# Selective scan: two of sixteen states take their product with B from GpSimd instead of VectorE

## The chip, the core and the metric

The kernel runs on one core of a Trainium2 chip. The metric is the device time of one execution in microseconds (us); less is better.

## The reference

Four layers, each a mixer and a feed-forward part with residuals, on four images of 64 x 64 positions and 96 channels. Layer 0 has a gated recurrence of its own. Layers 1 to 3 share a selective scan over four orders of the positions (row by row, column by column, and both backwards), 192 inner channels and 16 states per channel. Cut to what the change touches:

```python
# per layer 1..3; xs: [image, 4 orders, 192 channels, 4096 positions]
dts, B, C = split(x_proj(xs))            # B, C: 16 rows for each order, the same for all channels
delta = softplus(dt_proj(dts) + bias)
for t in range(4096):                    # for every image, order, channel and state n
    h[n] = exp(delta[t] * A[n]) * h[n] + (delta[t] * u[t]) * B[n, t]
    y[t] = sum_n(h[n] * C[n, t])
y = y + D * u
```

Afterwards the four orders are added, normalised, gated with silu(z) and projected out; the feed-forward part works in an 8-bit float format.

## The kernel before

**Stages.** Layer 0 runs first (function `gated`, to about 1800 us). Then `scans` works through 12 stages (4 images x 3 layers), and at the end the last image's output part runs alone. The work between two scans of an image (projections, convolution, norms, feed-forward) is cut into small steps by generators (`between`, `Job`, `Chain`), which the scan loop pumps beside its own work.

**Tiles of the scan.** A stage has two directions, four segments of T = 1024 positions each, and three chunks; a chunk fills 128 partitions with 64 channels of one order and 64 channels of another. So there are 12 x 2 x 4 x 3 = 288 chunks (`Item`), each with 16 states: 4608 state tiles of 128 x 1024 in float32. The list `tiles` holds them in order, and the loop over k takes one state a step.

**One state on the engines.**
- ScalarE: `decays` writes `da = exp(delta * A[n])` to SBUF (three buffers), two states ahead.
- TensorE: `b_rows` spreads B's row n over the partitions, two matmuls of a selection matrix `sel` with `bs` (B in three bfloat16 parts), into the PSUM tile `bc` from `wide()` (two buffers), one state ahead.
- VectorE, in `scan`: a product `bc = du * bc` in place (`du = delta * u`), then `beside()`, which pumps the other work, then the scan instruction `h <- da, carry, bc`.
- SyncE: `c_rows` starts two transfers that spread C's row out of the DRAM tile `cs` over 64 partitions each, two states ahead, into one of six buffers `c`.
- ScalarE: `carry` saves the last column of h. GpSimd: `times_c` makes `c = h * c`, one state behind.
- TensorE: `accumulate`, three states behind, adds h * C into the PSUM tile `acc`, which sums the 16 states of a chunk; `keep_busy` fills TensorE with idle matmuls (`nothing`) up to 1536 columns a step. `take` copies a full `acc` out on ScalarE four states behind the last state, that is in the step of state 3 of the next chunk, ahead of that step's other ScalarE work.

**Order.** Every engine is wrapped in `InOrder`: its instructions run in the order in which the program issues them. Within a step the order is `take`, `carry`, `c_rows`, `decays`, `logarithms` (at state 11), `b_rows`, `times_c`, `scan` with `beside`, `store`, `accumulate`. `logarithms` takes the logarithm of all variances that wait in `pending`; with the exponentials around it that costs ScalarE a table load before and one after. `prepare_chunk` makes delta (softplus, at state 4) and du (on GpSimd) of the next chunk; `prepare_segment` makes the rows of B and C, every third chunk, and stores C's rows to `cs`.

**Buffers.** PSUM holds two `bc` tiles of two banks, two banks for the other work and `acc` with two. The SBUF tile `e` is used in layer 0 alone.

All instructions carry the line of the wrapper `InOrder.call` in the profile (L91), so groups are told apart by their tiles.

Of the kernel before, what the change touches and what calls it, by code (L numbers as in the profile page):

```python
# [10 lines left out]
F32 = mybir.dt.float32  # L11
# [4 lines left out]
ALU = mybir.AluOpType  # L16
# [5 lines left out]
NS = 16  # L22
# [3 lines left out]
T = 1024  # L26
MM = 512
# [11 lines left out]
NC2 = 2 * NS  # L39
# [26 lines left out]


FILL = 1536


def columns(lhs, rhs, place):
# [45 lines left out]
def metaformer(ctx: ExitStack, tc: tile.TileContext, x, l0_ab, l0_rest, ssm, ffn, out):  # L117
    nc = tc.nc
    pe, act, dve, pool, sp = (
        InOrder(tc, e) for e in (nc.tensor, nc.scalar, nc.vector, nc.gpsimd, nc.sync)  # L120
    )
# [3 lines left out]
    dram = ctx.enter_context(tc.tile_pool(name="dram", bufs=6, space=bass.MemoryType.DRAM))  # L125
    pbc = ctx.enter_context(tc.tile_pool(name="pbc", bufs=2, space=bass.MemoryType.PSUM))

    def sb(bufs, tag, shape, dtype=F32):
        return pools[bufs].tile(shape, dtype, tag=tag, name=tag)

    def const(name, shape, dtype=F32):
        return pools[1].tile(shape, dtype, name=name)
# [3 lines left out]
    def wide():  # L136
        return wides[0].tile([128, T], F32, tag="bc", name="bc")
# [4 lines left out]
    def bank(name):  # L142
        banks["free"] -= 1
        return banks["pool"].tile([128, MM], F32, tag="ps", name=name)

    def release():
        banks["back"] += 1

    def settle():
        banks["free"] += banks["back"]  # L150
        banks["back"] = 0
# [16 lines left out]
    def drain(chain, others=lambda: None, until=lambda: False):  # L168

        while chain is not None and not chain.done and not until():  # L170
            if not pump(chain):
                others()
            settle()
# [41 lines left out]
    for layer in range(4):  # L215
# [8 lines left out]
        b = const(f"b_{layer}", [128, 3 + C])  # L224
# [558 lines left out]
    def load_segment(item):  # L783
        sg = Segment()
        t = slice(item.seg * T, (item.seg + 1) * T)
        sg.steps = False
        sg.us = [sb(4, "u", [128, T]) for _ in range(3)]
        for c in range(3):
            sp.dma_start(out=sg.us[c], in_=item.im.u[c, :, t])
        weights[item.layer].load_xp()  # L790
        sg.bs = sb(2, "bs", [NB3, T], BF16)
        sg.cs = dram.tile([NC2, T], F32, tag="cs", name="cs")
        return sg

    def prepare_segment(item, sg):

        xp = weights[item.layer].xp
        rows = sg.rows = sb(1, "rows", [128, T])
        for k in range(2):
            cols = slice(k * MM, (k + 1) * MM)  # L800
            ps = bank("x_proj")
            for c in range(3):
                o = (3 * item.d + c) * XPW
                pe.matmul(
                    ps[0:XPW], xp[:, o : o + XPW], sg.us[c][:, cols], start=c == 0, stop=c == 2
                )
                if c:
                    yield

            bs = sg.bs[:, cols]  # L810
            act.copy(rows[0:XPW, cols], ps[0:XPW])
            sg.steps = k == 1
            act.copy(bs[0:32], ps[0:32])
            yield
            rem = rows[64:96, cols]
            dve.tensor_tensor(rem, ps[0:32], bs[0:32], ALU.subtract)
            release()
            yield
            for p in (32, 64):
                act.copy(bs[p : p + 32], rem)  # L820
            yield k == 0
        sp.dma_start(out=sg.cs, in_=rows[NC2 : 2 * NC2])
        pool.tensor_tensor(sg.bs[64:96], rows[64:96], sg.bs[64:96], ALU.subtract)

    def prepare_chunk(item):
# [33 lines left out]
    def scans(stages, jobs, pac):  # L859
# [10 lines left out]
        sg = load_segment(items[0])  # L870
# [4 lines left out]
        tiles = [(i, n) for i in items for n in range(NS)]  # L875
        last = len(tiles) - 1
        live = {}
# [3 lines left out]
        def start(i):  # L881
# [2 lines left out]
                pool.memset(carries[i.chunk], 0.0)  # L884
            i.carry = carries[i.chunk]

        def c_rows(k):
            i, n = tiles[k]
            c = live[k, "c"] = sb(6, "c", [128, T])
            for half in range(2):  # L890
                row = NS * half + n
                sp.dma_start(
                    out=c[64 * half : 64 * half + 64],
                    in_=i.sg.cs[row : row + 1, :].to_broadcast([64, T]),
                )

        def decays(k):
            i, n = tiles[k]
            da = live[k, "da"] = sb(3, "da", [128, T])
            at = (3 * i.d + i.chunk) * NS + n  # L900
            act.activation(da, i.delta, AF.Exp, scale=weights[i.layer].decay[:, at : at + 1])

        def b_rows(k):
            i, n = tiles[k]
            b = live[k, "b"] = wide()
            for half in range(2):
                cols = slice(half * MM, (half + 1) * MM)
                pe.matmul(
                    b[:, cols], sel[:, n, :], i.sg.bs[:, cols], start=True, stop=True
                )  # L910

        def scan(k, beside):
            i, n = tiles[k]
            da, b = live.pop((k, "da")), live.pop((k, "b"))
            dve.tensor_tensor(b, i.du, b, ALU.mult)
            beside()
            h = live[k, "h"] = sb(3, "h", [128, T])
            step = slice(None, None, -1 if i.d else 1)
            dve.tensor_tensor_scan(
                h[:, step],  # L920
                da[:, step],
                b[:, step],
                initial=i.carry[:, n : n + 1],
                op0=ALU.mult,
                op1=ALU.add,
            )
# [49 lines left out]
        def take(i):  # L976
            i.y = sb(2, "y", [128, T])
            act.copy(i.y, i.acc)
# [15 lines left out]
        decays(0)  # L994
        decays(1)
        b_rows(0)
        working = []

        def work():

            while working and working[0].done:
                working.pop(0)
            if working:
                working[0].step()

        for k in range(last + 5):
            q, n = divmod(k, NS)
            if k <= last:
                item = items[q]
                nxt = at(q + 1)  # L1010
                if n == 0:
                    if q % per == 0:
                        item.im.y = dram.tile([3, 128, L], F32, tag="y", name="y")
                        working += jobs[q // per]
                    if item.chunk == 2:
                        drain(segment, work, lambda: nxt.sg.steps)
                    chain = Chain(prepare_chunk(nxt), True) if nxt is not None else None
                if item.chunk == 1 and n == 4 and at(q + 2) is not None:
                    if q % per == per - 2:
                        for job in jobs[q // per][:1]:  # L1020
                            while not job.done:
                                work()
                                settle()
                    segment = Chain(next_segment(items[q + 2 : q + 5]))
                if n == 8 and nxt is not None:
                    start(nxt)
                if n == 8 and nxt is not None and nxt.d == 1:
                    nxt.yf = sb(2, "y", [128, T])
                    sp.dma_start(out=nxt.yf, in_=nxt.im.y[nxt.chunk, :, nxt.seg * T : (nxt.seg + 1) * T])
            def beside():  # L1030
                pump(chain)
                pump(segment)
                if n == 13:
                    drain(chain, work)
                    if item.chunk == 2:
                        drain(segment, work)
                work()

            full = items[(k - 4) // NS] if k >= 4 and (k - 4) % NS == NS - 1 else None
            if full is not None:  # L1040
                take(full)
            if 0 <= k - 1 <= last:
                carry(k - 1)
            if k + 2 <= last:
                c_rows(k + 2)
                decays(k + 2)
            if n == 11:
                logarithms()
            if k + 1 <= last:
                b_rows(k + 1)  # L1050
            if 0 <= k - 1 <= last:
                times_c(k - 1)
            before = pe.columns
            if k <= last:
                scan(k, beside)
            if full is not None:
                store(full)
            if 0 <= k - 3 <= last:
                fill = max(0, FILL - int(pe.columns - before)) // MM
                if tiles[k - 3][1] == NS - 1:  # L1060
                    keep_busy(tiles[k - 3][0], fill)
                accumulate(k - 3)
                if tiles[k - 3][1] < NS - 1:
                    keep_busy(tiles[k - 3][0], fill)
            settle()
# [380 lines left out]
```

## Time and profile before

| | |
|---|---|
| median of three runs | 19232.42 us (19219.73 to 19237.42) |
| the profiled execution | 19237.79 us, its span 19236.0 us |
| VectorE busy | 17678.3 us, 92% |
| TensorE matmuls busy | 15881.9 us, 83% |
| GpSimd busy | 13540.9 us, 70% |
| ScalarE busy | 11070.3 us, 58% |
| DMA | 3192.77 MB, mean 166 GB/s |
| mean granted TensorE clock | 0.906 |

A group of the profile reads: engine, operation, written tile <- read tiles, partitions x elements, count | busy time in us, mean duration of one in ns | idle time of the engine just ahead of them, and what ended it. PE is TensorE, PEld its weight loads, DVE VectorE, ACT ScalarE, POOL GpSimd, SP SyncE. The table by stretches gives for each engine busy us and number of instructions, then the granted clock of TensorE, the busy share of the DMA engines and GB/s. In the timeline a row has start and duration in us; what is in brackets is the idle time before it and who ended it.

### The profile page before, as it was taken

What the parts mean: (1) busy time and instruction counts of PE and PEld (TensorE: products, weight loads), DVE (VectorE), ACT (ScalarE), POOL (GpSimd) and SP (SyncE); (2) the same over time, 40 slices, a digit from 0 to 9 for tenths busy, and PEclk for the clock granted to TensorE, in tenths of its full rate; (3) what the DMA queues carried; (4) which work ended last, traced back from release to release, by engine and by line L of the source; (5) the groups of instructions that cost most, each with busy time, mean ns of one, the idle gap of its engine ahead of it and who ended that gap; (6) DMA issues with size and microseconds to landing.
All of it is one profiled execution on the core that took longest, in us unless ns stands there. A gap on an engine that the chain in (4) does not pass through costs nothing.

```text
span 19236.0 us, 231374 instructions
## 1 busy us (share of the span) xinstructions
PE 15881.9 (83%) x75043; PEld 4903.2 (25%) x75043; DVE 17678.3 (92%) x13768; ACT 11070.3 (58%) x17831; POOL 13540.9 (70%) x9223
## 2 busy tenths in 40 slices
PE   8998787787787888888887888887887888788887
PEld 3332121121122222222222222222222222223333
DVE  6757999999999999999999999999999999999995
ACT  3544564564555665665665665665665665666664
POOL 3434777777777777777777777777777777777775
PEclk9999999998999899898899898899898898898887
DMA  1213676676676667666667677667666676676674
GB/s 50 54 45 86 165 190 174 169 190 170 170 189 178 172 186 185 173 186 184 172 186 183 171 190 184 170 188 187 170 192 181 169 194 179 170 196 176 171 182 114
DMA packets 1269891, 3192.77 MB, mean 166 GB/s; under 512 B 440336, under 2 KB 440560, under 8 KB 1262544
## 3 DMA queue, kind: packets, MB, share of 16 engines
q1 hardware_dynamic: 1268688, 3177.97, 62.4%
q8 instruction: 604, 9.90, 0.2%
q14 instruction: 599, 4.91, 0.1%
HBM read 2818.51 MB, written 308.28 MB: 163 GB/s over the span
## 4 chain that ended last, share of the span: by engine, by line
DVE 62%; PE 17%; ACT 10%; issue 4%; POOL 3%; DMA 2%; SPq 1%; DVEq 1%; POOLq 0%; ACTq 0%
DVE h L91 43%; DVE bc L91 17%; ACT da L91 5%; PE acc L91 5%; PE bc L91 4%; ACT L91 2%; PE conv L91 1%; POOL c L91 1%; PE dt_proj L91 1%; DMA c<-cs 1%; PE c L91 1%; DVE st L91 1%; PE y_t L91 1%; POOL du L91 1%; SPq L91 1%
## 5 line engine op out<-in xcount | busy, mean ns | idle before, releaser
L91 POOL TENSOR_TENSOR c<-h,c 128x1024 f32<-128x1024 f32 (+1 forms) x4992 | 11344.4, 2275 | 5043.9 <-DVE h L91 3032.8
L91 DVE TENSOR_TENSOR_SCAN h<-da,carry,bc 128x1024 f32<-128x1024 f32 x4608 | 10796.2, 2343 | 543.1 <-POOL c L91 38.1
L91 ACT ACTIVATE da<-delta,decay 128x1024 f32<-128x1024 f32 x4608 | 5286.8, 1148 | 1696.4 <-DVE h L91 1689.8
L91 DVE TENSOR_TENSOR bc<-du,bc 128x1024 f32<-128x1024 f32 x4608 | 5563.1, 1207 | 187.9 <-PE bc L91 177.2
L91 PE MATMUL acc<-c,twice 64*64 64x512 f32 x36864 | 5586.9, 679 | 27.0 <-POOL c L91 27.0
L91 PE MATMUL bc<-bs,sel 96*128 96x512 bf16 x9216 | 3042.3, 415 | 2801.7 <-DVE h L91 2729.7
L91 ACT COPY carry<-h 128x1 f32<-128x1 f32 x3456 | 653.2, 189 | 3983.4 <-DVE h L91 3980.3
L91 PEld LDWEIGHTS <-sel 96*128 96x128 bf16 x9216 | 593.7, 100 | 6162.0 <-DVE h L91 5068.6
L91 PE MATMUL acc<-sel,nothing 96*128 96x512 bf16 x5795 | 1728.8, 404 | 0.0
L91 PEld LDWEIGHTS acc<-c,twice 64*64 64x64 f32 x36864 | 1060.0, 142 | 2460.7 <-issue 1897.0
L91 ACT ACT_TABLE_LOAD x1287 | 1651.2, 1283 | 37.9 <-DVE mv L91 20.0
L91 PEld LDWEIGHTS <-nothing 96*128 96x128 bf16 x5795 | 417.7, 100 | 2143.5 <-issue 1957.9
L91 PE MATMUL conv<-pad,tap_lo 128*128 128x512 f32 x1728 | 880.8, 615 | 0.0
L91 PE MATMUL dt_proj<-rows,w 12*128 12x512 f32 x1152 | 747.5, 732 | 6.8 <-ACT delta L91 4.3
L91 ACT COPY y<-acc 128x1024 f32<-128x1024 f32 x288 | 291.6, 1013 | 762.3 <-PE acc L91 750.7
L91 POOL TENSOR_TENSOR du<-delta,u 128x1024 f32<-128x1024 f32 x288 | 679.3, 2359 | 1.5 <-issue 1.5
L91 ACT ACTIVATE c<-c,l_bias 128x512 f32<-128x512 f32 x384 | 263.6, 686 | 673.4 <-PE c L91 670.7
L91 PE MATMUL x_proj<-u,xp 128*108 128x512 f32 x1152 | 587.1, 619 | 19.0 <-DMA xp<-in_ssm 9.3
L91 PE MATMUL conv<-pad,tap_hi 128*128 128x512 f32 (+1 forms) x1152 | 602.6, 626 | 0.0
L91 DVE TENSOR_TENSOR_SCAN h<-da,l_carry,bc 128x512 f32<-128x512 f32 x384 | 491.3, 1280 | 41.9 <-DVE bc L91 1.4
L91 PE MATMUL bc<-rows,u 96*128 96x512 f32 x768 | 399.1, 645 | 42.5 <-DVE h L91 42.5
L91 PE MATMUL bc<-xp,u 96*128 96x512 f32 x768 | 395.5, 640 | 25.9 <-DVE h L91 25.9
(146 smaller groups left out, 12895.3 us busy)
## 6 DMA issues: line engine op xcount, KB each, us to landing
c<-cs SPq DMA_DIRECT2D x9216, 256.0 KB, 4.2
u<-u SPq DMA_DIRECT2D x288, 512.0 KB, 6.8
y<-y SPq DMA_DIRECT2D x1152, 128.0 KB, 3.5
y<-y SPq DMA_DIRECT2D x144, 512.0 KB, 6.1
xr<-x SPq DMA_DIRECT2D x224, 192.0 KB, 5.0
u<-u SPq DMA_DIRECT2D x288, 128.0 KB, 3.8
pad<-y SPq DMA_DIRECT2D x288, 128.0 KB, 4.7
z<-zl SPq DMA_DIRECT2D x96, 256.0 KB, 4.6
```

The lines of the kernel that those rows point to most:

```text
L91: ins = f(*a, **k).ins
```

## The change

States 4 and 12 of every chunk (`ON_POOL`) go another way. B's rows are stored to `cs` too, which is twice as large. For these states SyncE spreads B's row out of DRAM into the SBUF tile `e` (one buffer), five states ahead (`b_from_dram`); GpSimd multiplies it with du in place (`times_b_on_pool`), two states ahead and behind the product with C of that step; ScalarE writes the decay to a PSUM tile from `wide()`, in the place that `bc` had, one state ahead and behind the next state's decay (and at state 11 behind the logarithms); the broadcast matmuls and VectorE's product are gone. The scan reads its decay from PSUM and its product from SBUF. In the step before such a state the columns that `keep_busy` fills up to are 1024 fewer.

```diff
--- before.py
+++ after.py
@@ -66,6 +66,7 @@
 
 
 FILL = 1536
+ON_POOL = (4, 12)
 
 
 def columns(lhs, rhs, place):
@@ -789,7 +790,7 @@
             sp.dma_start(out=sg.us[c], in_=item.im.u[c, :, t])
         weights[item.layer].load_xp()
         sg.bs = sb(2, "bs", [NB3, T], BF16)
-        sg.cs = dram.tile([NC2, T], F32, tag="cs", name="cs")
+        sg.cs = dram.tile([2 * NC2, T], F32, tag="cs", name="cs")
         return sg
 
     def prepare_segment(item, sg):
@@ -819,7 +820,7 @@
             for p in (32, 64):
                 act.copy(bs[p : p + 32], rem)
             yield k == 0
-        sp.dma_start(out=sg.cs, in_=rows[NC2 : 2 * NC2])
+        sp.dma_start(out=sg.cs, in_=rows[0 : 2 * NC2])
         pool.tensor_tensor(sg.bs[64:96], rows[64:96], sg.bs[64:96], ALU.subtract)
 
     def prepare_chunk(item):
@@ -884,19 +885,35 @@
                 pool.memset(carries[i.chunk], 0.0)
             i.carry = carries[i.chunk]
 
+        def on_pool(k):
+            return 0 <= k <= last and tiles[k][1] in ON_POOL
+
+        def rows_of(i, first, dst):
+            for half in range(2):
+                row = first + NS * half
+                sp.dma_start(
+                    out=dst[64 * half : 64 * half + 64],
+                    in_=i.sg.cs[row : row + 1, :].to_broadcast([64, T]),
+                )
+
         def c_rows(k):
             i, n = tiles[k]
             c = live[k, "c"] = sb(6, "c", [128, T])
-            for half in range(2):
-                row = NS * half + n
-                sp.dma_start(
-                    out=c[64 * half : 64 * half + 64],
-                    in_=i.sg.cs[row : row + 1, :].to_broadcast([64, T]),
-                )
+            rows_of(i, NC2 + n, c)
+
+        def b_from_dram(k):
+            i, n = tiles[k]
+            b = live[k, "b"] = sb(1, "e", [128, T])
+            rows_of(i, n, b)
+
+        def times_b_on_pool(k):
+            i, n = tiles[k]
+            b = live[k, "b"]
+            pool.tensor_tensor(b, i.du, b, ALU.mult)
 
         def decays(k):
             i, n = tiles[k]
-            da = live[k, "da"] = sb(3, "da", [128, T])
+            da = live[k, "da"] = wide() if on_pool(k) else sb(3, "da", [128, T])
             at = (3 * i.d + i.chunk) * NS + n
             act.activation(da, i.delta, AF.Exp, scale=weights[i.layer].decay[:, at : at + 1])
 
@@ -912,7 +929,8 @@
         def scan(k, beside):
             i, n = tiles[k]
             da, b = live.pop((k, "da")), live.pop((k, "b"))
-            dve.tensor_tensor(b, i.du, b, ALU.mult)
+            if not on_pool(k):
+                dve.tensor_tensor(b, i.du, b, ALU.mult)
             beside()
             h = live[k, "h"] = sb(3, "h", [128, T])
             step = slice(None, None, -1 if i.d else 1)
@@ -994,6 +1012,7 @@
         decays(0)
         decays(1)
         b_rows(0)
+        b_from_dram(ON_POOL[0])
         working = []
 
         def work():
@@ -1043,14 +1062,21 @@
                 carry(k - 1)
             if k + 2 <= last:
                 c_rows(k + 2)
-                decays(k + 2)
+                if not on_pool(k + 2):
+                    decays(k + 2)
+            if on_pool(k + 5):
+                b_from_dram(k + 5)
             if n == 11:
                 logarithms()
-            if k + 1 <= last:
+            if on_pool(k + 1):
+                decays(k + 1)
+            elif k + 1 <= last:
                 b_rows(k + 1)
             if 0 <= k - 1 <= last:
                 times_c(k - 1)
-            before = pe.columns
+            if on_pool(k + 2):
+                times_b_on_pool(k + 2)
+            before = pe.columns - (2 * MM if on_pool(k + 1) else 0)
             if k <= last:
                 scan(k, beside)
             if full is not None:
```

## The prediction

> **What bounds the kernel now.** I read the page first, for which engine is full and for how long:
>
> ```profile
> PE 15881.9 (83%) x75043; PEld 4903.2 (25%) x75043; DVE 17678.3 (92%) x13768; ACT 11070.3 (58%) x17831; POOL 13540.9 (70%) x9223
> DVE  6757999999999999999999999999999999999995
> ```
>
> VectorE is at 90% or more in every slice from the fifth to the last but one. The table by stretches, cut at the first product with B (1807 us) and the last scan (19032 us), isolates that stage:
>
> ```profile
> core 0: us, PE busy (x) PEld busy (x) DVE busy (x) ACT busy (x) POOL busy (x), PEclk, DMA share, GB/s
> 1807.00:19032.00 17225.00, 14127.37 (x70023) 4171.92 (x70023) 16468.27 (x11914) 10139.75 (x15885) 12785.04 (x7895) 0.91 0.68 179
> ```
>
> VectorE works 16468 of 17225 us there (95.6%). Third, the groups with shapes kept apart: busy time, mean ns of one, idle time before.
>
> ```profile
> L91 DVE TENSOR_TENSOR_SCAN h<-da,carry,bc 128x1024 f32<-128x1024 f32 x4608 | 10796.2, 2343 | 543.1 <-POOL c L91 38.1 <-ACT da L91 8.8 <-DVE bc L91 5.2
> L91 DVE TENSOR_TENSOR bc<-du,bc 128x1024 f32<-128x1024 f32 x4608 | 5563.1, 1207 | 187.9 <-PE bc L91 177.2 <-PE dt_proj L91 7.4
> L91 POOL TENSOR_TENSOR du<-delta,u 128x1024 f32<-128x1024 f32 x288 | 679.3, 2359 | 1.5 <-issue 1.5
> L91 ACT ACTIVATE da<-delta,decay 128x1024 f32<-128x1024 f32 x4608 | 5286.8, 1148 | 1696.4 <-DVE h L91 1689.8
> L91 DVE SCALAR_TENSOR_TENSOR da<-bc,l_bias,delta 128x512 f32<-128x512 f32 x256 | 189.6, 740 | 189.7 <-PE bc L91 187.5 <-DMA delta<-c 2.2
> ```
>
> The first two rows are a state's step: 1.207 + 2.343 = 3.55 us of 3.74. VectorE idles 543 us ahead of scans (118 ns each, the hand-over from the product) and 188 ahead of products; the other engines wait for it. So the stage is as long as VectorE's work.
>
> **Gross gain.** 288 chunks of a segment with two states each lose 576 products: 576 x 1.207 = 695 us. On GpSimd the product is the form of du<-delta,u (third row, three SBUF operands): 576 x 2.359 = 1359 us, which brings GpSimd to 14144 of some 16900 us, 84%: not a bound by its sum.
>
> **The scan itself.** It now takes its decay from PSUM and its product from SBUF, the reverse of before. No scan of that kind is in the trace; the last row above has that placement (first tensor PSUM, second SBUF) at 740 ns, its sister bc<-bc,l_bias,du, written to PSUM, takes 759. Hence 0 +- 40 ns per 1024 columns, +- 23 us in all; I take 0.
>
> **Where ScalarE gives half of it back.** Decays were written two states ahead; for states 4 and 12 the PSUM buffer allows one state ahead only, behind the next state's decay in ScalarE's queue, and the scan before is not followed by a product that would cover it. A chunk in the timeline (rows of other engines left out), first state 3, then state 11:
>
> ```profile
> 17511.74 2.35 DVE L91 TENSOR_TENSOR_SCAN h<-da,carry,bc 128x1024 f32<-128x1024 f32 x1
> ...
> 17515.95 1.01 ACT L91 COPY y<-acc 128x1024 f32<-128x1024 f32 x1 [4.20 <-PE acc L91]
> ...
> 17516.96 1.15 ACT L91 ACTIVATE da<-delta,decay 128x1024 f32<-128x1024 f32 x1
> ...
> 17519.95 2.33 DVE L91 TENSOR_TENSOR_SCAN h<-da,carry,bc 128x1024 f32<-128x1024 f32 x1
> ...
> 17542.76 2.33 DVE L91 TENSOR_TENSOR_SCAN h<-da,carry,bc 128x1024 f32<-128x1024 f32 x1
> ...
> 17545.22 1.15 ACT L91 ACTIVATE da<-delta,decay 128x1024 f32<-128x1024 f32 x1
> ...
> 17546.38 1.28 ACT L91 ACT_TABLE_LOAD   x1
> ...
> 17547.90 1.28 ACT L91 ACT_TABLE_LOAD   x1
> ...
> 17549.98 2.35 DVE L91 TENSOR_TENSOR_SCAN h<-da,carry,bc 128x1024 f32<-128x1024 f32 x1
> ```
>
> State 3: ScalarE waits for TensorE's last sum of the chunk before, copies it out, then writes the decay of state 5, done at 18.11. State 4's decay now follows it, done at 19.26. Without its product VectorE could start scan 4 at 19.95 - 1.21 = 18.74: late by 0.5 to 0.6 us with the hand-over. Taken so through the 285 chunks that are whole in the trace, the scan of state 4 starts earlier by 0.47 us on average, not 1.207: 288 x 0.47 = 135 us kept. Another 33 us come back one product later, since VectorE now waited for the broadcast matmuls of state 5 at times, and TensorE has one pair (0.60 us) less ahead of them.
>
> State 11: the pending logarithms (two table loads, 1.28 each) now lie ahead of state 12's decay; they lay behind it. It would be ready at 17549.2 + 1.15 = 50.35, VectorE at 48.77: the scan comes later than before by 0.4 us. 99 of the 285 chunks have logarithms there and lose 0.235 us on average; the other 186 gain 1.093. Kept: 186 x 1.093 - 99 x 0.235 = 180 us.
>
> Sum so far: 135 + 33 + 180 = 348, of 695.
>
> **Small terms.** The 118 ns hand-over vanishes where the scan does not wait for ScalarE, about half: +34. GpSimd's product stands ahead of the products with C of states 2 and 10, which come up to 2.36 us later; its idle gaps absorb that within two to four states. Carried through every chunk, a product with C ends too late for the reuse of its h buffer in few: -18, I take -20. VectorE waits for broadcast matmuls 130 times today (177.2 us); arriving 0.6 us early it would lose up to 130 x 0.6 = 78 there: -40.
>
> **At nothing.** 1152 transfers of 256 KB (c<-cs: landing 4.2 us) are issued three states, some 11 us, before use; the DMA share goes from 0.68 to about 0.75, and SyncE, which issues one in 0.54 us, idles 9327 us waiting for c buffers. If that cover goes, GpSimd waits and C follows: the same kind of wait costs it 308 us today and VectorE 38. The cs rows written double, 96 transfers of 256 instead of 128 KB (3.7 us to landing; zl<-z, 256 KB, takes 4.6): 0.9 us under the 8 us or more until first use. ScalarE writing to PSUM is in no row; 128x1024 activations and copies lie between 1.013 (y<-acc) and 1.148 us, so 0 to 0.13 shorter, up to 40 us of gain where it is late; I take 0. The Trainium skill, "PSUM — Partial Sum Buffer", Specifications, says ScalarE writes faster to PSUM than to SBUF; by it the sum would gain something of that.
>
> **TensorE's clock.** The change removes 1152 broadcast matmuls and, as the new program's order shows, 593 of 5795 fillers. In a light stretch what is left of such a state is 1.09 (accumulation) + 0.27 (one filler) of 3.55 us, 38%. The trace says what that does:
>
> ```profile
> 17542.20:17545.60 3.40, 1.69 (x14) 0.52 (x7) 3.40 (x5) 0.48 (x2) 3.40 (x4) 1.00 0.95 235
> 17545.60:17549.00 3.40, 3.40 (x17) 1.98 (x15) 3.40 (x7) 3.35 (x4) 2.33 (x2) 0.53 0.38 93
> ```
>
> After a window with TensorE half busy, the granted clock is half; of full-clock windows below 50% busy, 162 of 163 were followed so. At half clock a state costs 1.03 + 1.98 + 1.33 = 4.34 us of TensorE, 0.8 too much, with 2.9 us of slack before a product waits, 1.7 after state 4: at most 288 x 0.2 = 58 us, I take -20. The Trainium skill, "TensorE: Matmul & The Clock Gate", in its closing table, asks only that no gap between bursts exceed about 3 us; by that rule no clock is lost here and the term is 0. The window above, busy for half of its time, speaks for the row.
>
> Sum: 348 + 34 - 20 - 40 - 20 = 302 us. The profiled execution took 19237.8 us (span 19236.0), 5.4 above the median of 19232.4; from the median, 18930.
>
> **Rivals.** (1) ScalarE's lateness hides, because it writes PSUM faster and TensorE, relieved, finishes the old sum earlier: only state 12's logarithms cost, 168 lost of 695, and 695 - 168 + 34 - 80 = 481 saved, 18750; without any loss 18500. Against: 273 of 288 copies of y wait for TensorE, 750.7 us. (2) GpSimd's detour reaches ScalarE: the norm steps behind it come up to 2.36 us later, and ScalarE waits in line for them 119 times today (192.6 us). Were each to grow so, 281 us would go, and the result lie at 19210, no change. For: ScalarE has 1 us of slack at states 4 and 12. Against: most of those waits lie in states 5 to 9 and 13 to 15, where decays have some 7 us. (3) Slower: VectorE's second tensor, so far in PSUM, now comes from SBUF, and it and GpSimd hold each other up there. A scan then waits for the running GpSimd product, 0.84 x 2.36 / 2 = 0.99 us on average: 571 us on 576 scans against 302, 19500. It decides from 0.53 us per scan on. Against: the row at 740 ns has its second tensor in SBUF too, and the 37 of them that GpSimd covered whole took 734 ns, those that it left alone 744.
>
> **Numbers.** Forecast (18790 to 19100) 0.63; (1) 0.13; (2) 0.12; (3) 0.12. Range 18640 to 19230: it takes in most of (1) and (2) and leaves out (3). A measurement here can tell 0.2%, 38 us, from no change: faster by more 0.82 (forecast, (1), half of (2)), within 0.05, slower 0.13.
>
> **What would show it.** Right: DVE loses 576 products; ahead of the scans h<-bc,carry,e stands idle time released by ScalarE, 300 to 400 us in all, more at state 4 than at 12 but for chunks with logarithms; GpSimd at 82 to 86% of the stage; granted clock within 0.02 of 0.91. Wrong: those scans above 2.40 us or stretched under GpSimd's products (3); idle time released by POOL or PE over 100 us (2); hardly any released by ACT (1).

## The result and the profile after

The changed kernel takes 18926.08 us (median of four runs, 18915.09 to 18957.22); the kernel before, run beside it, 19227.49 us (19219.73 to 19237.42). The ratio is 0.9842 [0.983, 0.9854]: 301 us, 1.6%, faster. The forecast was 18930. The profiled execution took 18929.26 us with a span of 18927.5 us, 308.5 less than the span before.

The page of the changed kernel, busy time of the engines and VectorE's slices:

```profile
PE 15723.3 (83%) x73298; PEld 4864.4 (26%) x73298; DVE 17011.6 (90%) x13192; ACT 11009.1 (58%) x17831; POOL 14818.9 (78%) x9799
DVE  6757999999999999999999999999999999988885
```

VectorE has 576 instructions and 667 us of work less, and it still stands at 8 or 9 tenths in every slice of the scan. Of the 667 us 308 came off the span; the other 358 became idle time. The table by stretches for the scan stage, first product (1784 us) to last scan (18714 us):

```profile
core 0: us, PE busy (x) PEld busy (x) DVE busy (x) ACT busy (x) POOL busy (x), PEclk, DMA share, GB/s
1784.00:18714.00 16930.00, 13983.63 (x68271) 4139.46 (x68270) 15811.72 (x11344) 10083.50 (x15892) 14065.79 (x8474) 0.88 0.79 201
```

GpSimd is at 14066 of 16930 us, 83%. The granted clock fell from 0.91 to 0.88. (The stage of the kernel before runs from 1796 to 19021 us; the prediction cut it at 1807 and 19032, 11 us late at both ends, which leaves its length as it was, 17225.) The stage is 295 us shorter; the part ahead of it was 12 us shorter in this execution, though its instructions are the same.

Where the idle time stands is read from the groups with shapes kept apart: busy time, mean ns, idle time before and its releasers.

```profile
L92 DVE TENSOR_TENSOR_SCAN h<-da,carry,bc 128x1024 f32<-128x1024 f32 x4032 | 9448.4, 2343 | 479.5 <-POOL c L92 59.5 <-DVE bc L92 5.2 <-ACT da L92 2.9
...
L92 DVE TENSOR_TENSOR bc<-du,bc 128x1024 f32<-128x1024 f32 x4032 | 4872.1, 1208 | 258.8 <-PE bc L92 248.6 <-PE dt_proj L92 7.4
...
L92 POOL TENSOR_TENSOR e<-du,e 128x1024 f32<-128x1024 f32 x576 | 1358.9, 2359 | 0.6 <-DMA e<-cs 0.6
L92 DVE TENSOR_TENSOR_SCAN h<-bc,carry,e 128x1024 f32<-128x1024 f32 x576 | 1345.5, 2336 | 317.3 <-ACT bc L92 168.2 <-DMA c<-cs 91.8 <-issue 22.3
...
L92 ACT ACTIVATE bc<-delta,decay 128x1024 f32<-128x1024 f32 x576 | 638.0, 1108 | 103.2 <-DVE h L92 102.0
```

The new scans run as fast as the old (2336 against 2343 ns), and GpSimd's product takes what du takes (2359). But VectorE idles 317.3 us ahead of these 576 scans. The row puts 91.8 of that down to the transfer of C's row. Taken gap by gap it is ScalarE: of 218 gaps over 0.1 us, 214 (298 us) end within 150 ns after the end of the decay written to `bc`, whatever releaser is named; the other 4 (18.6 us) wait for GpSimd's product. State 4 has 199.0 us in 135 gaps, state 12 118.3 us in 83. Ahead of the products left, VectorE idles 258.8 us instead of 187.9, all but some 10 us of it behind TensorE's broadcasts.

The timeline (rows of other engines left out) shows one chunk's state 4, then its state 12:

```profile
17202.02 1.01 ACT L92 COPY y<-acc 128x1024 f32<-128x1024 f32 x1 [5.88 <-PE acc L92]
...
17203.02 1.15 ACT L92 ACTIVATE da<-delta,decay 128x1024 f32<-128x1024 f32 x1
...
17204.07 1.11 ACT L92 ACTIVATE bc<-delta,decay 128x1024 f32<-128x1024 f32 x1
...
17205.27 2.35 DVE L92 TENSOR_TENSOR_SCAN h<-bc,carry,e 128x1024 f32<-128x1024 f32 x1 [0.61 <-issue]
...
17233.54 1.28 ACT L92 ACT_TABLE_LOAD   x1
...
17235.06 1.28 ACT L92 ACT_TABLE_LOAD   x1
...
17236.36 1.12 ACT L92 ACTIVATE bc<-delta,decay 128x1024 f32<-128x1024 f32 x1
...
17237.57 2.35 DVE L92 TENSOR_TENSOR_SCAN h<-bc,carry,e 128x1024 f32<-128x1024 f32 x1 [1.67 <-ACT bc L92]
```

At state 4 ScalarE copies out the old sum when TensorE has it ready, writes state 5's decay, then state 4's, which ends at 17205.18; the scan starts 0.09 us later, after 0.61 us of idle time named "issue". At state 12 the two table loads stand ahead of the decay, and VectorE idles 1.67 us.

VectorE's waits that stand ahead of products and scans in the stage (us in total, times, longest):

```profile
DVE bc L92 <- PE bc L92: 248.6, 163, 6.4
DVE h L92 <- ACT bc L92: 168.2, 98, 4.1
DVE h L92 <- DMA c<-cs: 91.8, 79, 5.9
DVE h L92 <- POOL c L92: 71.7, 27, 11.6
...
DVE st L92 <- DMA xr<-x: 27.2, 14, 4.5
...
DVE h L92 <- POOL e L92: 18.6, 4, 8.3
```

There are 163 waits for a broadcast instead of 130. GpSimd's two rows make 90 us, where products with C alone cost 38; but 12.2 of the 71.7 us stand ahead of the new scans, in gaps that end with ScalarE's decay. That leaves 78 us for GpSimd. The row of xr<-x, a transfer of the other work, was 0.2 us before the change.

### The profile page after: what moved, and what is told of

It reads as the page before. It is cut to its first block, busy times and chain, and to the rows that moved or that the text cites. A ratio compares the mean times of both kernels' runs of the same rounds, so it can differ in the third digit from the quotient of the medians.

```text
span 18927.5 us, 231165 instructions
## 1 busy us (share of the span) xinstructions
PE 15723.3 (83%) x73298; PEld 4864.4 (26%) x73298; DVE 17011.6 (90%) x13192; ACT 11009.1 (58%) x17831; POOL 14818.9 (78%) x9799
## 5 line engine op out<-in xcount | busy, mean ns | idle before, releaser
L92 DVE TENSOR_TENSOR_SCAN h<-da,carry,bc 128x1024 f32<-128x1024 f32 x4032 | 9448.4, 2343 | 479.5 <-POOL c L92 59.5
L92 PE MATMUL acc<-c,twice 64*64 64x512 f32 x36864 | 5705.3, 693 | 45.5 <-POOL c L92 45.4
L92 ACT ACTIVATE da<-delta,decay 128x1024 f32<-128x1024 f32 x4032 | 4619.4, 1147 | 1196.3 <-DVE h L92 1190.9
L92 DVE TENSOR_TENSOR bc<-du,bc 128x1024 f32<-128x1024 f32 x4032 | 4872.1, 1208 | 258.8 <-PE bc L92 248.6
L92 PE MATMUL bc<-bs,sel 96*128 96x512 bf16 x8064 | 2722.3, 423 | 2310.1 <-DVE h L92 2255.4
L92 PE MATMUL acc<-sel,nothing 96*128 96x512 bf16 x5202 | 1641.9, 419 | 0.0
L92 DVE TENSOR_TENSOR_SCAN h<-bc,carry,e 128x1024 f32<-128x1024 f32 x576 | 1345.5, 2336 | 317.3 <-ACT bc L92 168.2
L92 POOL TENSOR_TENSOR e<-du,e 128x1024 f32<-128x1024 f32 x576 | 1358.9, 2359 | 0.6 <-DMA e<-cs 0.6
L92 ACT ACTIVATE bc<-delta,decay 128x1024 f32<-128x1024 f32 x576 | 638.0, 1108 | 103.2 <-DVE h L92 102.0
L92 PE MATMUL x_proj<-u,xp 128*108 128x512 f32 x1152 | 661.9, 688 | 31.3 <-DMA xp<-in_ssm 14.1
```

The lines of the kernel that those rows point to most:

```text
L92: ins = f(*a, **k).ins
```

## Experiments

All edits are to the changed kernel. Times are medians; ratios stand against the kernel before, run beside each (medians 19234.55 to 19235.62 us; for the change itself 19227.49).

| kernel | what it does | us | ratio |
|---|---|---|---|
| the change | | 18926.08 | 0.9842 [0.983, 0.9854] |
| e1_first | decay of states 4 and 12 ahead of the next state's decay and of the logarithms on ScalarE | 18860.35 | 0.9805 [0.9792, 0.9819] |
| e2_fill | the 593 fillers are back | 18921.21 | 0.9837 [0.9824, 0.9851] |
| e5_comp | more fillers than before in place of the broadcast | 18926.65 | 0.9836 [0.9823, 0.985] |
| e9_pace | e5 and a matmul that waits where the broadcast did | 18930.83 | 0.9844 [0.983, 0.9857] |
| e3_sbuf | the decay stays in SBUF | 19173.54 | 0.9968 [0.9956, 0.9979] |
| e4_detour | GpSimd's work alone, VectorE's products stay | 19278.23 | 1.0023 [1.0014, 1.0032] |
| e6_first_comp | e1 and e5 | 18824.84 | 0.9787 [0.9774, 0.9801] |
| e7_late | e6 with states 9 and 15 | 18849.82 | 0.98 [0.9787, 0.9814] |
| e8_three | e6 with states 4, 10 and 15 | 18745.94 | 0.9746 [0.9732, 0.9759] |
| e10_three_pace | e8 with the waiting matmul | 18692.13 | 0.9718 [0.9705, 0.9732] |

Layer 0 is the same work in all of them, and yet the scan's first product starts between 1777 and 1799 us in the profiled executions. A difference of some 20 us between two of them can lie there.

### Is it ScalarE's place in the queue? (e1_first)

My theory was the prediction's: the lateness of ScalarE takes back nearly half. The rival: take it away, and another engine is the next one late.

```diff
             if k + 2 <= last:
                 c_rows(k + 2)
+                if on_pool(k + 1):
+                    decays(k + 1)
                 if not on_pool(k + 2):
                     decays(k + 2)
...
-            if on_pool(k + 1):
-                decays(k + 1)
-            elif k + 1 <= last:
+            if not on_pool(k + 1) and k + 1 <= last:
                 b_rows(k + 1)
```

> The change, with the decay of states 4 and 12 issued on ScalarE ahead of the next state's decay and ahead of the logarithms. Theory (half of the gain goes to ScalarE's late decays; the scans of states 4 and 12 waited 199 and 118 us in all): the decay comes 1.15 us earlier at state 4, and 1.15 us and two table loads earlier at state 12, so of 317 us of waits some 60 stay, all at state 4: 18926 - 250 = 18680. Rival (TensorE, late and at half clock around these states, takes what ScalarE gives back): the waits ahead of these scans go, but products wait for TensorE's broadcast instead, and less than 80 us come: above 18850.

The kernel's groups, products and scans from GpSimd's product:

```profile
L92 DVE TENSOR_TENSOR bc<-du,bc 128x1024 f32<-128x1024 f32 x4032 | 4872.4, 1208 | 369.9 <-PE bc L92 360.2 <-PE dt_proj L92 7.4
...
L92 DVE TENSOR_TENSOR_SCAN h<-bc,carry,e 128x1024 f32<-128x1024 f32 x576 | 1342.0, 2330 | 103.6 <-ACT bc L92 72.2 <-POOL e L92 19.2 <-POOL norm L92 3.4
```

ScalarE's part came true: the idle time ahead of these scans fell from 317.3 to 103.6 us (state 4: 199 to 84, state 12: 118 to 19). But 111 us of it came up again ahead of products: the waits for broadcasts at state 5 rose from 40 to 93 us, at state 14 from 67 to 92, at state 15 from 11 to 31. The time fell by 66 us, not by 214: it is the rival's (above 18850) and not the theory's 18680, while the scans' waits fell much as the theory said. ScalarE is what is late first, TensorE what is late next.

### What happened to TensorE? (e2_fill, e5_comp, e9_pace)

The prediction had put a loss of clock down to fewer fillers. So the fillers were put back (e2), then more of them in place of the broadcast (e5):

```diff
-            before = pe.columns - (2 * MM if on_pool(k + 1) else 0)
+            before = pe.columns                                        # e2
+            before = pe.columns + (2 * MM if on_pool(k + 1) else 0)    # e5
```

> The change, with the fillers of the step before states 4 and 12 put back (593 more, up to 1536 columns as in all other steps). Theory (these light steps cost TensorE its clock: granted 0.66 at state 12 against 0.91 before the change, and VectorE waits 60 us more for the broadcast at state 14): the granted clock at state 12 rises to 0.8 or more, the wait at state 14 falls by 30 to 50 us: 18880. Rival (the fillers stand in TensorE's queue ahead of the broadcast of the state after, which the short state needs 1.2 us sooner): products of states 5 and 13 wait more, 18930 to 18980.

> The change, with more fillers in the step before states 4 and 12 than elsewhere: up to 2560 columns, so that they stand in for the broadcast matmuls that are gone. Putting back the 593 fillers alone had raised the granted clock at state 12 only from 0.66 to 0.70 and moved the time by nothing clear. Theory (the light step costs TensorE its clock, and the slow TensorE delays the broadcast of state 14): now the clock at state 12 comes to 0.85 or more, the wait ahead of state 14's product falls from 0.23 us on average to 0.12 or less, and the time by 30 to 50 us: 18885. Rival (the clock is no cause; the crowd of other matmuls at states 13 and 14 is, met 1.2 us earlier): the clock rises, the wait stays, 18920 to 18950.

Neither moved the time (18921.21 and 18926.65 us). The mean granted clock during state 12 was 0.91 before the change and 0.66 after it; the fillers brought it to 0.70 and 0.74, short of the 0.8 and 0.85 that the theories gave, and the wait ahead of state 14's product stayed at some 240 ns. The reason is in the table by stretches of the changed kernel, one chunk's states 10, 11, 12 and 13:

```profile
core 0: us, PE busy (x) PEld busy (x) DVE busy (x) ACT busy (x) POOL busy (x), PEclk, DMA share, GB/s
11390.60:11394.20 3.60, 3.54 (x22) 0.84 (x22) 3.47 (x3) 1.15 (x1) 3.47 (x2) 1.00 0.62 139
11394.20:11397.80 3.60, 0.18 (x1) 0.00 (x0) 3.47 (x4) 2.19 (x2) 3.52 (x2) 0.90 1.01 247
11397.80:11400.05 2.25, 2.19 (x10) 0.43 (x10) 2.25 (x3) 1.15 (x1) 2.11 (x1) 0.50 0.13 26
11400.05:11403.60 3.55, 3.55 (x13) 0.88 (x13) 3.45 (x3) 0.00 (x0) 2.56 (x2) 0.50 0.31 100
```

TensorE is busy for all of state 10 and idle for nearly all of state 11; then it works states 12 and 13 at half the clock. Its rows in the timeline of the same stretch say why:

```profile
11392.96 1.09 PE L92 MATMUL acc<-c,twice 64*64 64x512 f32 x8
...
11393.99 0.39 PE L92 MATMUL acc<-sel,nothing 96*128 96x512 bf16 x1
...
11397.86 1.03 PE L92 MATMUL bc<-bs,sel 96*128 96x512 bf16 x2 [3.49 <-DVE h L92]
...
11398.83 1.99 PE L92 MATMUL acc<-c,twice 64*64 64x512 f32 x8
```

The broadcast for state 12 would have stood in step 11 and waited there for the scan of state 10, whose `bc` it overwrites. With it gone nothing holds TensorE: it runs step 11's accumulation and fillers beside the scan of state 10, as far as its data are there, and then waits 3.49 us for state 13's broadcast, behind the scan of state 11. Fillers of step 11 run ahead in the same way, before the gap and not in it. On average over the chunks (a state from the end of the scan before to the end of its own) TensorE is busy for 94% of state 10 and 27% of state 11, where it was 69% and 76%. In 145 of the 288 chunks it stands still for over 3 us on end in state 11, and the mean clock of state 12 is 0.54 there; in 97 it stands still for 2 to 3 us, with 0.73. The Trainium skill, "TensorE: Matmul & The Clock Gate", in its closing table, asks that no gap between bursts exceed about 3 us, and says that one brings the slow clock back; the 3.49 us and the 0.50 behind them agree. But the gap is not all: in the scan stage after the change, 332 windows of 3.4 us at full clock had TensorE busy for less than half, 322 of them were followed by half clock, and in 140 of these no gap of over 3 us stood. The prediction's row, a window below half busy, covers both kinds.

So e9 puts a wait in the place of the broadcast's: one small matmul with a matrix of zeros (`idle`), which adds to the sum and reads the h that the scan of state 10 writes. Its condition holds for state 12 and not for state 4, where the sum that it would add to has not been started. The fillers of e5 stay in.

```diff
+        def pace(k):
+            i, n = tiles[k - 3]
+            if 0 < n < NS - 1:
+                pe.matmul(i.acc[:, 0:64], idle, live[k - 1, "h"][:, 0:64], start=False, stop=False)
...
                 b_rows(k + 1)
+            if on_pool(k + 1):
+                pace(k)
```

> The change with fillers up to 2560 columns (run before: 18927, clock 0.735 at state 12), and one small matmul of zeros more, on TensorE in the step before state 12, where the broadcast matmuls stood; it reads the h of the state before and so waits for that scan, as the broadcast's buffer did. Theory: the fillers did nothing because TensorE, without the broadcast to wait for, runs the step's work ahead, beside the scan before (TensorE is busy 97% of the time in state 10 and 21 to 36% in state 11), and then idles for some 3 us until the next broadcast's buffer comes free; so with the wait back the clock at state 12 comes to 0.85 or more. If the clock is what makes the product of state 14 wait (0.24 us on average), that wait falls to 0.15 or less and the time to 18880. Rival (the crowd of the next segment's matmuls at states 13 and 14, met 1.2 us earlier, makes it wait whatever the clock): the clock comes back, wait and time stay: 18910 to 18940.

The same stretches of this kernel, states 10 to 13:

```profile
core 0: us, PE busy (x) PEld busy (x) DVE busy (x) ACT busy (x) POOL busy (x), PEclk, DMA share, GB/s
11408.40:11412.00 3.60, 2.38 (x13) 0.53 (x13) 3.47 (x4) 1.15 (x1) 3.46 (x2) 1.00 0.59 172
11412.00:11415.60 3.60, 2.64 (x15) 0.91 (x15) 3.47 (x4) 2.19 (x2) 3.52 (x2) 1.00 0.50 141
11415.60:11417.85 2.25, 2.18 (x13) 0.63 (x14) 2.25 (x3) 1.15 (x1) 2.11 (x1) 1.00 0.63 153
11417.85:11421.40 3.55, 2.42 (x14) 0.52 (x12) 3.44 (x4) 0.00 (x0) 2.58 (x2) 1.00 0.62 156
```

The work is even again, the clock is full in this chunk and 0.90 on average in state 12, and the stage's time at half clock, from first product to last scan, is 3093 us (3131 before the change, 3970 after it, 3540 in e5). So the wait that went with the broadcast is what the clock of e5 lacked; whether the waiting matmul would do it without e5's fillers was not run. The time did not follow, as the rival had it: 18930.83 us. The wait ahead of state 14's product fell from 243 (e5) to 161 ns a chunk, that ahead of state 13's rose from 22 to 77: what the full clock gives at one state, the new wait mostly takes at the one before.

### Does the placement in PSUM matter? (e3_sbuf)

The prediction's rival of VectorE and GpSimd holding each other up was not seen. This kernel leaves the decays of states 4 and 12 in SBUF, two states ahead like the others, so that both of a scan's tensors come from SBUF.

```diff
-            da = live[k, "da"] = wide() if on_pool(k) else sb(3, "da", [128, T])
+            da = live[k, "da"] = sb(3, "da", [128, T])
...
-                if not on_pool(k + 2):
-                    decays(k + 2)
+                decays(k + 2)
...
-            if on_pool(k + 1):
-                decays(k + 1)
-            elif k + 1 <= last:
+            if not on_pool(k + 1) and k + 1 <= last:
```

> The change, but the decay of states 4 and 12 stays in SBUF and is written two states ahead as before, so that the scan reads both of its tensors from SBUF. If VectorE and GpSimd don't hold each other up: scans stay at 2.34 us, ScalarE is never late, 18926 - 317 = 18610 or a little more. If they do (the page SBUF of the Trainium skill, section Who interferes with whom, says that an instruction of VectorE with two SBUF inputs contends with one of GpSimd that reads SBUF): such a scan waits for the running GpSimd product, or that for the scan, up to 2.36 us and about 1 us on average: 576 us are lost against 317 gained, 19190.

Its groups: GpSimd's product with C, the two kinds of scan and VectorE's product between them:

```profile
L92 POOL TENSOR_TENSOR c<-h,c 128x1024 f32<-128x1024 f32 x4608 | 11600.1, 2529 | 1873.3 <-DVE h L92 1045.9 <-DMA c<-cs 286.5 <-issue 279.6
L92 DVE TENSOR_TENSOR_SCAN h<-da,carry,bc 128x1024 f32<-128x1024 f32 x4032 | 9447.5, 2343 | 498.2 <-POOL c L92 64.6 <-ACT da L92 6.3 <-DVE bc L92 2.4
...
L92 DVE TENSOR_TENSOR bc<-du,bc 128x1024 f32<-128x1024 f32 x4032 | 4870.0, 1208 | 416.9 <-PE bc L92 408.1 <-PE dt_proj L92 7.5
...
L92 DVE TENSOR_TENSOR_SCAN h<-da,carry,e 128x1024 f32<-128x1024 f32 x576 | 1694.4, 2942 | 18.5 <-POOL e L92 18.5
```

No scan waits for ScalarE any more (18.5 us, all GpSimd), and yet the kernel is 247 us slower than the change. The scan takes 2942 ns on average: half of them up to 2.43 us, a quarter above 3.18, one in a hundred above 6.70. That is 349 us more on the scans (1694.4 against 1345.5), about what the waits for ScalarE had cost (317.3 to 18.5), and the products wait 158 us more for TensorE, which is again the next one late. GpSimd's products with C grow as well, 2529 ns against the 2358 of the change's own row:

```profile
L92 POOL TENSOR_TENSOR c<-h,c 128x1024 f32<-128x1024 f32 x4608 | 10830.2, 2358 | 2451.9 <-DVE h L92 1508.3 <-DMA c<-cs 308.7 <-issue 282.1
```

Instruction by instruction the two meet: the 135 of these scans that start while GpSimd is idle take 2342 ns on average, the 161 that start with over 1 us of a GpSimd instruction to go take 3856 (2342 in the change); the 825 products with C that overlap such a scan take 3310 ns, all others 2359. So the collision exists in this kernel, with two tensors in SBUF, and does not show with one of the two in PSUM. The Trainium skill, "SBUF — State Buffer", "Who interferes with whom", says so for VectorE instructions with two SBUF inputs, since the second comes through a port shared with GpSimd; these rows agree. The kernel's time is close to the 19190 that was expected for this case.

### What does the detour alone cost? (e4_detour)

The transfers and the products on GpSimd are made and not used; states 4 and 12 go as before the change.

```diff
         def on_pool(k):
+            return False
+
+        def aside(k):
             return 0 <= k <= last and tiles[k][1] in ON_POOL
...
-            if on_pool(k + 5):
+            if aside(k + 5):
                 b_from_dram(k + 5)
...
-            if on_pool(k + 2):
+            if aside(k + 2):
                 times_b_on_pool(k + 2)
```

> The kernel before, with the transfers of B's rows and GpSimd's products for states 4 and 12 added and their results left unused: TensorE's broadcast and VectorE's product stay for all states. It prices what the change adds, without what it takes away. Theory: GpSimd's idle time takes the 1359 us in; VectorE loses 20 to 60 us to late products with C and norms: 19250 to 19290. Rival (GpSimd's detour reaches ScalarE's queue and so the scans): 200 to 300 us slower, 19430 to 19530.

Groups of this kernel:

```profile
L92 DVE TENSOR_TENSOR_SCAN h<-da,carry,bc 128x1024 f32<-128x1024 f32 x4608 | 10798.5, 2343 | 555.7 <-POOL c L92 52.6 <-ACT da L92 6.8 <-DVE bc L92 3.4
...
L92 DVE TENSOR_TENSOR bc<-du,bc 128x1024 f32<-128x1024 f32 x4608 | 5565.4, 1208 | 225.6 <-PE bc L92 215.7 <-PE dt_proj L92 7.5
```

44 us slower than before: 19278.23 us, within the theory's range. In the profiled execution, with 19311.09 us the slowest of eleven, waits for GpSimd's products with C are 15 us longer and those for broadcasts 38, though TensorE's work is what it was. The detour is cheap, but twice what the prediction gave it.

### Which states, and how many? (e6_first_comp, e7_late, e8_three, e10_three_pace)

e6 joins e1 and e5. e7 takes states 9 and 15 in place of 4 and 12, away from the copy of the old sum and from the logarithms; e8 takes three states, none of them 12; e10 adds the matmul of e9 to e8, ahead of states 10 and 15.

```diff
-ON_POOL = (4, 12)
+ON_POOL = (9, 15)          # e7
+ON_POOL = (4, 10, 15)      # e8, e10
```

> The early decays of the first experiment (18860) and the fillers of the run above together. In the first experiment the scans' waits fell by 213 us, but products waited 111 us more for TensorE's broadcasts, at states 5, 14 and 15. Theory (the part at 14 and 15 is the clock's): those two fall by 0.3 us together, 90 us in all, 18770 to 18800. Rival (no cause): 18850 to 18870.

> As the run above, but with states 9 and 15 in place of 4 and 12: behind them TensorE's broadcast was early before the change (it ended more than 2 us after its buffer came free in a tenth of the chunks or less; at state 5 in four tenths), and ScalarE copies no sum out ahead of them. Theory (what is lost besides ScalarE is the place where VectorE arrives too early for TensorE): waits of products stay near the 188 us of before, 18650 to 18720. Rival (a gain ahead of states 0 to 4, where TensorE is over 90% busy, is lost there): products of states 1 to 5 wait more and the time stays at 18780 to 18860.

> As the run above, but with three states a chunk: 4, 10 and 15. GpSimd takes 680 us more and comes to 90% of the stage, the DMA share to 0.84. If VectorE's work is still what counts: 288 x 1.2 = 347 us less, of which a half to two thirds stay as before: 18450 to 18550. If GpSimd or TensorE bound the stage by then: products with C late, scans waiting for their h buffer or for GpSimd's product over 150 us in all, no better than with two states: 18650 to 18800.

> Three states a chunk (4, 10, 15; 18746) with that small matmul in the steps before states 10 and 15. If the clock costs time: waits of products, 434 us in all, fall by 50 to 100 us, 18650 to 18700. If not: 18730 to 18760.

e6 gave 18824.84 us, 36 less than e1, between its two expectations. What the fillers did there is not shown: the waits at states 14 and 15 fell by 49 and 50 ns a chunk against e1, but state 5's rose by 96, and of the 38 us between the two profiled executions 20 lie ahead of the scan stage. e7 was 25 us slower than e6, in its rival's range: the waits that the late states avoid come back as steps that are longer than in the kernel before, at states 0 to 3 (by 68, 117, 147 and 34 ns a chunk) and 10 to 12 (121, 100, 73). e8 is faster by 79 us than e6 with a third product gone, against some 350 us of VectorE's work, which is its rival's range too; its products wait 434 us. e10 shows where some of that lay. Its groups, products and scans from GpSimd's product:

```profile
L92 DVE TENSOR_TENSOR bc<-du,bc 128x1024 f32<-128x1024 f32 x3744 | 4524.0, 1208 | 362.0 <-PE bc L92 352.6 <-PE dt_proj L92 7.4
...
L92 DVE TENSOR_TENSOR_SCAN h<-bc,carry,e 128x1024 f32<-128x1024 f32 x864 | 2016.2, 2334 | 176.8 <-ACT bc L92 92.2 <-POOL e L92 66.9 <-DMA c<-cs 4.4
```

Its stretch from 1800 to 18450 us:

```profile
core 0: us, PE busy (x) PEld busy (x) DVE busy (x) ACT busy (x) POOL busy (x), PEclk, DMA share, GB/s
1800.00:18450.00 16650.00, 13944.08 (x70598) 4313.69 (x70598) 15468.01 (x11052) 10046.24 (x15888) 14696.03 (x8757) 0.92 0.84 213
```

The products' waits are down to 362 us, the clock at 0.92 (0.89 in e8), and the time at 18692.13 us, as its theory had it and 54 less than e8, with no run of the one inside the range of the other. It is the fastest version, 2.8% under the kernel before. GpSimd is at 88% of that stretch and the transfers at 0.84; scans now wait 67 us for GpSimd's product.

## Why the prediction was right

The time (18930 against 18926) and the mechanism came out: VectorE is the bound, its work falls by the products (667 us), and ScalarE, late with the decay, takes back nearly half (299). That the sum of small terms fits as well is partly luck, errors that cancel: ScalarE's part came out 115 us smaller than predicted, and the other terms together 109 us worse. In the span of the profiled executions:

| term, us | predicted | measured |
|---|---|---|
| VectorE's products gone | -695 | -667 |
| their hand-over gone, 118 ns each, and other idle ahead of the old scans | -68 | -85 |
| idle ahead of the new scans, by ScalarE | +414 | +299 |
| idle ahead of products, by TensorE | +27 | +71 |
| waits for GpSimd, ahead of scans | +20 | +40 |
| idle ahead of VectorE's other work, 27 of it for xr<-x | 0 | +34 |
| sum | -302 | -308 |

(The predicted +414 is the 380 lost, 212 at state 4 and 168 at state 12, and the 34 of hand-over that was said to stay; +27 is -33, +40 and +20. The busy time of the page counts overlapping records once, hence 667 and not 695. GpSimd's +40 is 59.5 and 18.6 against 38.1.)

- **The gross gain** held: 2359 ns on GpSimd, 83% of the stage, no bound.
- **The scan itself**: -7 ns, inside +-40.
- **ScalarE** was the right engine at the right states, state 4 over state 12, just under the 300 to 400 us that were to be seen (299). Without their share of the hand-over 212 were predicted at state 4 and 168 at state 12; measured, with it and with 19 us of GpSimd's, 199 and 118. ScalarE's writes to PSUM are 40 ns shorter (1108 against 1147), in the direction of the Trainium skill's page that the prediction weighed ("PSUM — Partial Sum Buffer", Specifications), but over 576 decays that is 23 us at most: it explains part, and the rest of the error stays open.
- **TensorE** was priced too low, and one part of it had a wrong cause. The 33 us said to come back at state 5 were 6 (its wait went from 46 to 40 us). State 14's wait rose from 19 to 67 us and state 7's from 36 to 63, for which no step stood. The clock term had the right sign (0.906 to 0.883 over the execution, just beyond the 0.02 that the prediction allowed) by the wrong reason: not that a state without its broadcast is light, but that the wait of the broadcast is gone, and TensorE runs ahead and then stands still, for over 3 us in half of the chunks. The page's rule, by which the prediction said that the term would be 0, does bear on this case, through a gap that the prediction did not look for; the row that the prediction followed instead held as well. With two states, giving the clock back brought nothing net (e9); with three, the same matmul brought 54 us (e10).
- **GpSimd** was sized at 20 and measured at 40; as a detour whose products nobody uses it costs 44 (e4).
- **The transfers** were taken at nothing. C's rows bear that out: GpSimd waits 308.7 us for them where it waited 308.3. But VectorE waits 27 us for xr<-x, which no step of the prediction named; it is 10 us in the detour (e4) and 49 with three states (e10). Why these come too late stays open: their median time to landing rose only from 5.0 to 5.3 us. (The 4.6 us that the prediction gives for zl<-z are those of z<-zl; zl<-z takes 5.1, still under the 8 us of cover.)

The rivals: (1) had ScalarE's lateness hide but for the logarithms; it didn't, and when most of it was taken away (e1) TensorE took half of that: 18860, not 18750. (2) would have cost 281 us; e4 bounds all that the detour does at 44 where VectorE keeps its products. (3) did not occur: 2336 ns. Its mechanism is real (e3), but the row that was weighed against it, one tensor in PSUM and one in SBUF, was the right one to follow.

Left open: why state 14 waits. Its waits above 0.3 us after the change are 40, of which 27 are in a segment's second chunk, when the projections for the next segment are made. A crowded TensorE there is argued and not shown.

## What to carry to other kernels

Work taken off the engine that is the bound pays by what the next engines let through: for each place where it leaves, ask which instruction of another engine was covered by it, and place that one first in its queue (here 66 us for moving one line). An instruction that is removed takes its wait with it, and the wait may have been what kept another engine in step. Before giving a bound VectorE a second tensor from SBUF beside a busy GpSimd, keep one of the two in PSUM: the same change with both in SBUF brought 0.3% in place of 1.6%.

## What the runs showed of the hardware

- A scan with both tensors in SBUF beside a GpSimd at work took 2942 ns on average and 2.43 us in the median; with one in PSUM 2336 ns on average. The GpSimd products paid as well (2529 against 2358 ns).
- TensorE without a wait ran nearly a whole state ahead of VectorE (94% and 27% busy in neighbouring states), and after 3.49 us without a matmul its clock was 0.50 for the two states that followed. Gaps of 2 to 3 us there were followed by 0.73 on average, gaps of over 3 us by 0.54.
- Idle time ahead of a scan that waits for several engines was put down to a transfer (91.8 us) or to issue (22.3), while nearly every gap ended within 150 ns of the end of ScalarE's decay.
